# Attention with mixed heads: the products that form the softmax sums move from the front of a step's first mixing to its second quarter, and their reciprocals go behind the first transposition

## The chip, the cores and the metric

The kernel runs on one core of one Trainium2 chip. The metric is the device time of one execution in microseconds (us). The kernel before took 4113.27 us, the median of three runs that lie between 4112.35 and 4115.33 us.

## The reference, cut to what matters

Two attention layers work on x of shape 8 x 512 x 32 x 32, that is 8 images with 512 channels and 1024 positions. The change touches only the second layer:

```
q, k, v = w_q @ x, w_k @ x, w_v @ x            # 8 heads of 64 channels
attn = einsum('bhdq,bhdT->bhqT', q, k) * scale
attn = einsum('gh,bhqT->bgqT', w_head, attn)    # the heads are mixed
attn = softmax(attn, axis=-1)
mean, var = mean(attn), var(attn)               # over all queries and keys of a head
attn = (attn - mean) / sqrt(var + EPS) * in_gamma + in_beta
out  = einsum('bhqT,bhdT->bhqd', attn, v)       # then the projection w_proj
```

So for each query and head the kernel needs the sum of the exponentials (the softmax sum) and the sum of their squares (for var).

## The kernel before, in words

All data are float32. The first layer fills the span up to about 1800 us and is not touched. In the second layer the images follow one another, and each image has 8 blocks of 128 queries. A block passes through three stages, which lie in three successive steps; step p (p from 0 to 8, method `step`) works on three blocks at once and has four quarters, t = 0 to 3:

- Block p, scores (`scores`, L1631): eight products of queries and keys, two in each quarter. ScalarE copies each out of PSUM (L1643) into a tile `raw`, one tile for keys 0 to 511 (kh = 0) and one for keys 512 to 1023 (kh = 1). Then 16 DMAs of SyncE (`regroup`, L1648, 256 KB each) rearrange the rows into the tile `re`, so that all heads of 16 queries lie in 128 partitions. Slot s of `re` (s = 0 to 3) gets two DMAs for kh = 0 and two for kh = 1. They are issued in the order (kh, s) = (0,0), (0,1) in quarter 1, (0,2) in quarter 2, and (0,3), (1,0), (1,1), (1,2), (1,3) at the end of quarter 3. `re` has one buffer; `raw` has two.
- Block p-1, mixing (`mix`, L1665): four mixings, one a quarter, each 32 matmul records that read one slot of `re`. ScalarE takes the exponential of each in two halves into a tile `e` of 128 x 2048 (L1675; two buffers). VectorE transposes the tile (`flip`, L1687, into `et`) and takes mean and variance of each 512 columns (`moments`, four instructions of L1698). In quarter 3 the mixing stands ahead of the scores, in the other quarters behind them.
- Block p-2, values (`values`, L1714) from `et`: half 0 began in quarter 3 of the step before and ends in quarter 0; half 1 fills quarters 1 and 2. ScalarE moves each half out of PSUM (`leave`, L1730).

At the front of a step come the sums of block p-2. `sums` (three short VectorE instructions, L1740 to L1742) turns the 16 means and variances into the tile `zz`; its inputs are ready after the last `moments` of the step before. `totals` (L1749, two products, four matmul records) adds over the partitions into a PSUM tile `z`. `reciprocals` takes 1/z (L1760), keeps z (L1773), adds to the sum of squares (L1775 to L1780), and has GpSimd's queue write the reciprocals to DRAM (`zd`, L1763) and read them back spread over 64 partitions (`rzb`, L1770, 256 KB). GpSimd uses `rzb` two blocks later (`divide`, L1802).

The order of the work is written out by hand: every engine runs its instructions in the order in which the program emits them. On TensorE quarter 0 is thus: scores 0 and 1, second half of values half 0, `totals`, mixing 0. On VectorE: `sums`, `reciprocals`, `flip` 0, `moments` 0. An agenda (`ag.run`) puts other work at places that are numbered 4p + t: the next image's normalization in step 5, parts of the next key projection in step 8, where there are no new scores.

PSUM of this layer has three tiles of two banks (`m_psum`, for scores and mixings, in turn) and two of one bank (`acc_psum`, for the halves of values and for `z`, in turn). `totals` is called once a block; seven of an image's eight calls lie in `step` (56 in all), the eighth after the loop, and that one is not changed.

Of the kernel before, what the change touches and what calls it, by code (L numbers as in the profile page):

```python
# [467 lines left out]
def tile_two_attention_layers(  # L468
# [795 lines left out]
    with ExitStack() as l1:  # L1264
# [180 lines left out]
        def k_leave():  # L1445
            for fn in due:
                fn()
            due.clear()
# [167 lines left out]
        class Attention1:  # L1616
# [221 lines left out]
            def step(self, p, t, ag):  # L1838

                new, old, older = p < NT, p >= 1, p >= 2  # L1840
                if t == 3 and old:
                    self.mix(p - 1, 3)
                if new:
                    self.scores(p, 2 * t)
                    if t == 0:
                        self.scores(p, 1)
                if t == 0 and older:
                    self.values(p - 2, 0, 2, 3)
                    self.leave(p - 2, 0)
                    self.sums(p - 2)  # L1850
                    if p % 2 == 0 and p >= 4:
                        self.divide(p // 2 - 2, nc.gpsimd)
                    self.totals(p - 2)
                if t in (1, 2) and older:
                    self.values(p - 2, 1, t - 1)
                if t == 3 and old:
                    self.values(p - 1, 0, 0)
                if new and t:
                    self.scores(p, 2 * t + 1)
                if t == 3 and old:  # L1860
                    self.values(p - 1, 0, 1)
                if t < 3 and old:
                    self.mix(p - 1, t)
                ag.run(4 * p + t - 0.5)
                if t == 2 and older:
                    self.values(p - 2, 1, 2, 3)
                    self.leave(p - 2, 1)
                k_leave()
                if old:
                    self.flip(p - 1, t)  # L1870
                    self.moments(p - 1, t)
                if new:
                    for kh, s in (
                        (), ((0, 0), (0, 1)), ((0, 2),), ((0, 3), (1, 0), (1, 1), (1, 2), (1, 3)),
                    )[t]:
                        self.regroup(kh, s)
                if old and t == 0:
                    self.piece(4 if p < 5 else 5)
                ag.run(4 * p + t)
# [155 lines left out]
```

## Time and profile before

| what | value |
|---|---|
| median of the runs shown | 4113.27 us |
| the profiled execution, time | 4113.24 us |
| its span, first to last instruction | 4111.1 us |
| TensorE matmul busy | 3950.6 us (96%) |
| VectorE busy | 2832.7 us (69%) |
| ScalarE busy | 1970.3 us (48%) |
| GpSimd busy | 128.8 us (3%) |
| mean granted TensorE clock | 0.991 |
| DMA, SyncE's queue (q1) | 43.1% of the 16 engines over the span |

A group line of the profile gives line, engine, operation, output and inputs, shapes and count, then busy time, mean duration of one in ns, and the idle time of the engine just before the group with what ended most of it. A matmul of float32 appears as two records. The time outside the span is 2.1 us in the profiled execution, and it agrees with the median to 0.03 us.

### The profile page before, as it was taken

What the parts mean: (1) busy time and instruction counts of PE and PEld (TensorE: products, weight loads), DVE (VectorE), ACT (ScalarE), POOL (GpSimd) and SP (SyncE); (2) the same over time, 40 slices, a digit from 0 to 9 for tenths busy, and PEclk for the clock granted to TensorE, in tenths of its full rate; (3) what the DMA queues carried; (4) which work ended last, traced back from release to release, by engine and by line L of the source; (5) the groups of instructions that cost most, each with busy time, mean ns of one, the idle gap of its engine ahead of it and who ended that gap; (6) DMA issues with size and microseconds to landing.
All of it is one profiled execution on the core that took longest, in us unless ns stands there. A gap on an engine that the chain in (4) does not pass through costs nothing.

```text
span 4111.1 us, 96037 instructions
## 1 busy us (share of the span) xinstructions
PE 3950.6 (96%) x41932; PEld 1825.8 (44%) x41932; DVE 2832.7 (69%) x4124; ACT 1970.3 (48%) x2431; POOL 128.8 (3%) x150
## 2 busy tenths in 40 slices
PE   8999999999999999999999999999999999999997
PEld 4353535353534344334534544444444445444344
DVE  4748485757575666648758768668678588587586
ACT  1717272636354444427427347257166175274373
POOL 0000000000000000000000001000000000000000
PEclk9999999999999999999999999999999999999998
DMA  3313131212121111138649559468287286386484
GB/s 129 106 51 109 49 114 44 88 47 88 47 81 45 58 69 65 68 102 216 182 113 219 150 142 220 131 165 218 95 204 201 93 217 173 119 215 190 107 197 121
DMA packets 268636, 519.12 MB, mean 126 GB/s; under 512 B 49840, under 2 KB 84912, under 8 KB 261552
## 3 DMA queue, kind: packets, MB, share of 16 engines
q1 hardware_dynamic: 261664, 497.96, 43.1%
q0 software_dynamic: 6544, 14.94, 1.6%
q8 instruction: 331, 5.42, 0.6%
q14 instruction: 97, 0.79, 0.1%
HBM read 197.16 MB, written 46.92 MB: 59 GB/s over the span
## 4 chain that ended last, share of the span: by engine, by line
PE 71%; DVE 21%; ACT 3%; issue 2%; DMA 2%; SPq 0%; DVEq 0%; ACTq 0%
PE s L1081 11%; PE a L1107 10%; DVE bn L1698 10%; DVE et L1687 9%; PE pk_p L899 5%; PE pq_p L899 5%; PE pv L1458 5%; PE pv_p L899 5%; PE pp_p L899 5%; PE pk L1383 4%; PE pq L1383 4%; PE pp L1383 4%; PE a L1714 4%; PE s L1631 4%; PE m L1665 2%
## 5 line engine op out<-in xcount | busy, mean ns | idle before, releaser
L1687 DVE STREAM_TRANSPOSE et<-e 128x2048 f32<-128x2048 f32 x256 | 589.6, 2303 | 179.3 <-ACT e L1675 175.6
L1714 PEld LDWEIGHTS a<-et,v 128*64 128x64 f32 x16384 | 515.0, 140 | 296.8 <-issue 278.3
L1698 DVE BATCH_NORM_STATS2 bn<-e 128x6 f32<-128x512 f32 x1024 | 635.4, 685 | 0.0
L1675 ACT ACTIVATE e<-m 128x1024 f32<-128x1024 f32 x512 | 496.5, 1021 | 248.5 <-issue 157.7
L1086 ACT ACTIVATE e<-s 128x1024 f32<-128x1024 f32 x512 | 497.2, 1026 | 233.6 <-PE s L1081 232.2
L1643 ACT COPY raw<-s 128x1024 f32<-128x1024 f32 x480 | 478.2, 1017 | 226.9 <-PE s L1631 204.9
L1714 PE MATMUL a<-et,v 128*64 128x64 f32 x16384 | 563.7, 226 | 9.5 <-DVE et L1687 5.2
L1631 PE MATMUL s<-k,q 64*64 64x512 f32 x4096 | 547.7, 620 | 9.4 <-DVE q L1497 3.1
L1094 DVE TENSOR_TENSOR zacc<-zacc,e 128x1024 f32<-128x1024 f32 x384 | 468.6, 1220 | 89.9 <-ACT e L1086 67.9
L1081 PE MATMUL s<-q,k 64*64 64x512 f32 x4096 | 490.1, 593 | 2.3 <-ACT e L1086 2.3
L1107 PE MATMUL a<-e,v 64*64 64x512 f32 x4096 | 484.1, 589 | 0.0
L1665 PE MATMUL m<-re,wmix 32*32 32x512 f32 x8192 | 335.2, 610 | 5.9 <-ACT e L1675 3.4
L1107 PEld LDWEIGHTS a<-e,v 64*64 64x64 f32 x4096 | 156.7, 133 | 282.8 <-issue 282.5
L1081 PEld LDWEIGHTS s<-q,k 64*64 64x64 f32 x4096 | 147.9, 133 | 275.2 <-issue 240.7
L1631 PEld LDWEIGHTS s<-k,q 64*64 64x64 f32 x4096 | 119.0, 133 | 259.8 <-issue 103.5
L1458 PE MATMUL pv<-wv,y 128*128 128x512 f32 x480 | 212.1, 597 | 0.0
L1730 ACT COPY q<-a 64x256 f32<-64x256 f32 x256 | 93.9, 367 | 175.1 <-PE a L1714 173.0
L1763 POOL DMA_DIRECT2D zd<-rz x56 | 34.7, 619 | 3471.5 <-DMA re<-raw 1854.1
L1458 PEld LDWEIGHTS pv<-wv,y 128*128 128x128 f32 x480 | 89.3, 190 | 117.5 <-issue 109.5
L1665 PEld LDWEIGHTS m<-re,wmix 32*32 32x32 f32 x8192 | 69.0, 103 | 147.7 <-ACT raw L1643 87.5
L1462 ACT COPY v<-pv 128x512 f32<-128x512 f32 x30 | 17.6, 586 | 218.4 <-PE pv L1458 218.4
L1749 PE MATMUL z<-sel,zz 128*32 128x32 f32 x256 | 30.5, 208 | 94.6 <-DVE zz L1740 81.3
(315 smaller groups left out, 3993.3 us busy)
## 6 DMA issues: line engine op xcount, KB each, us to landing
re<-raw SPq DMA_DIRECT2D x1024, 256.0 KB
left_q<-left_q SPq DMA_DIRECT2D x17, 1792.0 KB
left_p<-left_p SPq DMA_DIRECT2D x17, 1792.0 KB
left_k<-left_k SPq DMA_DIRECT2D x10, 1792.0 KB
x<-in_x_dram SPq DMA_DIRECT2D x32, 512.0 KB
rzb<-zd SPq DMA_DIRECT2D x128, 128.0 KB
x<-x SPq DMA_DIRECT2D x64, 256.0 KB
left_v<-left_v SPq DMA_DIRECT2D x8, 1792.0 KB
```

Source lines behind the costliest of these rows:

```text
L899: nc.tensor.matmul(out, st, mv, start=start, stop=(k == 1), skip_group_check=True)
L1081: nc.tensor.matmul(ps[c * D : c * D + D, m], k[r, hp, k0 : k0 + D], q[r, hp, ts(f, FB)], start=True, stop=True,)
L1086: nc.scalar.activation(e[i], ps, AF.Exp, scale=S0 * S0)
L1107: nc.tensor.matmul(acc[g][a][m * D : m * D + D], v[rows, kc, ts(2 * hp + m, D)], e[i][rows, m], start=(kc == 0), stop=(kc == NG - 1),)
L1383: nc.tensor.matmul(self.ps[m][:, i], w[:, left, k * HC + i * P : k * HC + i * P + P], right[:, k], start=(k == 0 and m != 2), stop=(k == 1 ...
L1458: nc.tensor.matmul(ps[:, m], y_t[b][:, c, ts(2 * i + m, P)], w[:, c], start=(c == 0), stop=(c == NCC - 1),)
L1631: nc.tensor.matmul(ps[c * D : c * D + D, m], qo_t[b][r, p, hp, ts(c, D)], k_t[b][r, hp, ts(kh, FB)], start=True, stop=True,)
L1665: nc.tensor.matmul(ps[a // 2][c * 32 : c * 32 + 32, a % 2].rearrange("p (r kb k) -> p r kb k", r=2, k=32), wmix[rows].rearrange("p g i -> ...
L1675: nc.scalar.activation(e[:, :, 2 * h : 2 * h + 2].rearrange("p r a k -> p a r k"), ps[h].rearrange("p a (r k) -> p a r k", r=2), AF.Exp,)
L1687: nc.vector.transpose(self.et[p, u].rearrange("p kb (r st a) g q -> p st kb r (a g q)", r=2, st=2)[:, st], self.e[p, s].rearrange("p r a ( ...
L1698: nc.vector.bn_stats(self.bn[p][:, s, a], e[:, :, a].rearrange("p r k -> p k r"))
L1714: nc.tensor.matmul(acc[two * D : two * D + D, s].rearrange("p (x q) -> p x q", q=4), v_t[b][:, kb, ts(g, D)], et[:, kb, :, g], start=(kb = ...
```

## The change

`totals`, with the reciprocals that it calls, leaves quarter 0. It is called in quarter 1, after the first part of values half 1. The `flip` and `moments` of mixing 0 leave quarter 0 as well: `flip` 0 now stands ahead of `totals`, and `moments` 0 behind it. In step 1, which has no block p-2, both stay where they were. `sums` stays in quarter 0.

```diff
                     self.sums(p - 2)
                     if p % 2 == 0 and p >= 4:
                         self.divide(p // 2 - 2, nc.gpsimd)
-                    self.totals(p - 2)
                 if t in (1, 2) and older:
                     self.values(p - 2, 1, t - 1)
+                    if t == 1:
+                        self.flip(p - 1, 0)
+                        self.totals(p - 2)
+                        self.moments(p - 1, 0)
                 if t == 3 and old:
                     self.values(p - 1, 0, 0)
...
-                if old:
+                if p == 1 or old and t:
                     self.flip(p - 1, t)
                     self.moments(p - 1, t)
```

The resulting orders: TensorE has scores 0 and 1, values, mixing 0, score 2, the first part of values half 1, `totals`, score 3, mixing 1. VectorE has `sums`, `flip` 0, the four or five instructions of `reciprocals`, `moments` 0, `flip` 1. GpSimd's two DMAs for the reciprocals follow `totals`. No instruction is added or removed; what an agenda place of quarter 0 gives VectorE now comes ahead of `flip` 0. The two `acc_psum` tiles are now taken in the order half 0, half 1, `z` instead of half 0, `z`, half 1.

## The prediction

> **What bounds the kernel now.** I read the page first, then who waited for whom on TensorE, then one undisturbed block in the timelines of TensorE and VectorE, and the sums of that stretch. From the page, the span, the engines and the group of the moved products:
>
> ```profile
> span 4111.1 us, 96037 instructions
> PE 3950.6 (96%) x41932; PEld 1825.8 (44%) x41932; DVE 2832.7 (69%) x4124; ACT 1970.3 (48%) x2431; POOL 128.8 (3%) x150
> ...
> L1749 PE MATMUL z<-sel,zz 128*32 128x32 f32 x256 | 30.5, 208 | 94.6 <-DVE zz L1740 81.3
> ```
>
> TensorE is idle for 160.5 us of the span (4111.1 - 3950.6), and 94.6 us of it lie ahead of these few products, which are themselves 30.5 us. The waits of TensorE:
>
> ```profile
> PE z L1749 <- DVE zz L1740: 81.3, 53, 3.3
> PE z L1749 <- DVE zz L1742: 13.2, 55, 0.2
> ...
> PE m L1665 <- DMA re<-raw: 1.6, 6, 0.4
> ```
>
> The last line is small (6 waits, 1.6 us), and it is the one to distrust: a regrouped row that lands while TensorE waits for `zz` shows no wait of its own. TensorE's timeline (start, duration, record, idle before it) across one block, its plain middle left out:
>
> ```profile
> 3340.32 0.25 PE L1749 MATMUL z<-sel,zz 128*32 128x32 f32 x2 [1.29 <-DVE zz L1740]
> 3340.81 0.25 PE L1749 MATMUL z<-sel,zz 128*32 128x32 f32 x2 [0.24 <-DVE zz L1742]
> 3340.99 1.14 PE L1665 MATMUL m<-re,wmix 32*32 32x512 f32 x32
> 3342.06 1.10 PE L1631 MATMUL s<-k,q 64*64 64x512 f32 x8
> ...
> 3359.79 2.08 PE L1714 MATMUL a<-et,v 128*64 128x64 f32 x64
> 3363.16 0.25 PE L1749 MATMUL z<-sel,zz 128*32 128x32 f32 x2 [1.29 <-DVE zz L1740]
> ```
>
> The period is 22.84 us (3363.16 - 3340.32), of which TensorE runs without a gap for 20.88 (3340.99 to 3361.87) and is held for 1.96. Many blocks have this period to 0.03 us, which a chain of latencies would do. VectorE's timeline shows the chain:
>
> ```profile
> 3344.31 2.31 DVE L1687 STREAM_TRANSPOSE et<-e 128x2048 f32<-128x2048 f32 x1 [2.23 <-ACT e L1675]
> 3346.54 2.49 DVE L1698 BATCH_NORM_STATS2 bn<-e 128x6 f32<-128x512 f32 x4
> ...
> 3362.92 0.19 DVE L1740 TENSOR_SCALAR zz<-bn 128x32 f32<-128x32 f32 x1
> ```
>
> From 3344.31 on it runs four pairs of transposition and moments without a gap, then `zz`; then the two products, mixing 0 behind them, its exponential, and only then the next transposition. VectorE idles 2.23 us for that exponential, and TensorE for VectorE. Neither is full: in this stretch VectorE is busy 20.11 of 22.85 us. The DMA engines are fuller. In the sums of the stretch the busy times of TensorE, its weight loads, VectorE, ScalarE and GpSimd follow its length; the last three numbers are the granted clock, the DMA share and GB/s:
>
> ```profile
> 3340.99:3363.84 22.85, 21.28 (x455) 11.00 (x453) 20.11 (x28) 16.90 (x20) 3.53 (x3) 1.00 0.89 219
> ```
>
> [...] mixing 0 had its data at 3339.48 and started at 3340.99, behind `z`. [...] the first regroup transfer of a step lands 3.24 us after its issue (median of 29) when GpSimd's spread of reciprocals is not in flight, 4.84 us (27) when it is. [...]
>
> **The change, part by part.** I use the 56 blocks whose products move. The held time runs from the end of values to the first record of mixing 0; landings come from the times at which each DMA's semaphore rises in the trace.
>
> 1. *The wait for `zz` goes.* Over the 56 blocks TensorE is held 120.8 us in all (2.16 a block, the products themselves included). What is late next is the second transfer of slot (1,0), which mixing 0 reads: it is issued 3.30 us before the end of values in steps 3 to 7, and lands 3.78 us (median; mean 4.03) after that, so about 0.5 us too late (0.45 in the block above: values end at 3339.03, the landing is at 3339.48). In the six blocks where it was the releaser, mixing 0 began 0.13 us after the landing. Block by block, held time less (landing + 0.13 - end of values): the landing alone would hold TensorE for 67.5 us. Removed: 120.8 - 67.5 = 53.3 us. In step 8, without new scores, little is won (0.6 a block), since values end earlier and the landing is about 2.9 us away.
>
> 2. *The products at their new place.* In an image's eighth block they have no gap before them, and take 0.24 us from their start to the next record (2035.04 to 2035.28). Bounds: 0.2, and 0.67 as in the timeline above. They push the scores, and so the landing: 56 x 0.24 = 13.4 us lost. Their wait for `zz` is over by 2 us: mixing, score and values (3.2 us) lie between. The PSUM tile they take now was emptied ahead of mixing 0.
>
> 3. *Reciprocals ahead of moments 0.* Five instructions, 0.98 us (3341.10 to 3342.08). They delay moments 0, transposition 1 and moments 1. Behind them waits the fourth exponential, which needs the tile that moments 1 frees. Moments 1 ends 12.67 us after mixing 0 begins, with the insert at 13.62; the exponential, ready at 12.98 + 0.24 = 13.22, starts near 13.72. Of this 0.5 us about half reaches the eighth score's copy (ScalarE has slack there, the score ends later anyway), and so the regroup. 48 blocks (steps 3 to 8) x 0.25 = 12 us lost; bounds 0 and 0.6 a block. VectorE waits for no product: `z` is done 3.6 us after mixing 0, transposition 0 ends at 5.55.
>
> 4. *GpSimd's two DMAs move with them.* The write now starts 5.5 us later relative to mixing 0 (recips at 5.6 for 0.11). The spread's packets are in flight from 8.75 to 11.3 us after mixing 0 (medians), and would be from 14.2 to 16.8. Before, they met slots (0,0) to (0,2), with time to spare; now they meet (0,3), issued at 13 to 13.8, ahead of (1,0), issued near 17.5. Between the landing of (0,3) (17.9) and of (1,0)'s first transfer (20.3) lie 2.4 us, of which one transfer takes 1.1 (the spacing of landings in a full queue), so 1.3 are free; so the median is covered, the late quarter is not. Bounds: 0, and 1.6 us, the measured slowing (4.84 - 3.24). I take 0.2 on average: 48 x 0.2 = 9.6 us.
>
> 5. *The rest costs nothing.* `zz` is computed where it was; GpSimd's multiply follows a step later; SyncE's queue issues the same in the same order. Agenda work that now precedes transposition 0 (0.8 us of normalization in step 5, two subtractions of 1.22 us in step 8) fits into VectorE's wait for the exponential or, in step 8, beside TensorE's key projection (3.63 us a product); without that cover it would cost its own duration, 8 x 0.8 and 8 x 2.4 us. Half 0 of values now takes the PSUM tile that half 1 leaves, which is empty 0.9 us before. ScalarE's fifth copy waits for the regroup of (1,3), which lands 6.2 to 8.1 us after that of (1,0); the copy comes 7.6 us after mixing 0, nearly always later.
>
> Sum: 53.3 - 13.4 - 12 - 9.6 = 18.3 us. Against the profiled execution, 4113.24 - 18.3 = 4094.9, say 4095 us; the median shown is 0.03 us away. The plain block would go from 22.84 to 20.88 + 0.24 + 0.58 + 0.25 + 0.2 = 22.15 us.
>
> **The rivals.** *Cover holds (chance 0.20).* Parts 3 and 4 cost nothing: 4113.24 - 53.3 + 13.4 = 4073. For: VectorE has 2 us free and ScalarE 6 of 22.85. Against: moments 1 is late by the instructions' own durations.
>
> *Traded (0.20).* The regroup takes what `zz` gives back; the engines at 0.89 get fuller in a shorter period. If the landing comes 0.36 us later still (17.3/48), 4112. For: landings over 5 us occur already. Against: (1,0) finds the queue nearly empty.
>
> *Slower (0.15).* The reciprocals' spread runs into (0,3) and (1,0). Each hit costs 1.6 us; without part 4 the gain is 27.9 us, so it decides at 17 of 48 blocks, and above 23 the loss passes 0.2%. With three quarters hit, 36 x 1.6 = 57.6, less 27.9: 4143. For: 0.89, and the measured slowing. Against: at 16.8 the packets are mostly done.
>
> That the change does not do what it says is excluded: the orders of instructions are as described.
>
> **How the numbers follow.** My forecast has 0.45, centre 4095, 4084 to 4105. About 0.2% (8 us) is what a measurement can tell here. Faster by more: 0.45 + 0.20 = 0.65; within: 0.20; slower: 0.15. The range runs from 4066 (the covered case with shorter landings) to 4122; it leaves out the slower case and a little at the low end, together under 0.2.
>
> **What would show it.** Right: the wait of `z` for `zz` gone; mixing 0 waiting for the DMA instead, some 1 us a block; VectorE idle near 1.5 us ahead of transposition 0 and none after it; plain periods of 21.9 to 22.4 us; the fourth exponential waiting for moments. Wrong: periods of 22.8 or above with (1,0) landing over 4.7 us after issue (part 4); TensorE idle ahead of scores or values (a PSUM tile I took as free); no DMA wait at mixing 0 and periods near 21.2 (part 1 too pessimistic).

## The result and the profile after

| | before | after |
|---|---|---|
| median | 4113.6 us (4112.35 to 4115.33, 4 runs) | 4056.8 us (4052.18 to 4059.13, 4 runs) |
| ratio, 95% interval | | 0.986 (0.9843 to 0.9877) |
| profiled execution, time | 4113.24 us | 4059.13 us |
| its span, mean granted clock | 4111.1 us, 0.991 | 4057.0 us, 0.993 |

The change takes off 56.8 us, where 18 were forecast. It went the way that was expected, and further than the range of the prediction reaches (4066 to 4122 us).

From the page of the kernel after: the span, the engines, and the group of mixings, whose last two numbers are the idle time ahead of it and what ended most of it.

```profile
span 4057.0 us, 96037 instructions
PE 3927.5 (97%) x41932; PEld 1817.7 (45%) x41932; DVE 2834.4 (70%) x4124; ACT 1969.0 (49%) x2431; POOL 128.7 (3%) x150
...
L1665 PE MATMUL m<-re,wmix 32*32 32x512 f32 x8192 | 334.9, 611 | 72.6 <-DMA re<-raw 60.7
```

Two things are to be seen. The idle time that stood ahead of `z` now stands ahead of the mixings, and is smaller (94.6 before, 72.6 here). And TensorE's *busy* time fell by 23.1 us (3950.6 to 3927.5) although it runs the same 41932 instructions. 10.5 us of that are the `z` products themselves, whose records now follow each other without a gap (busy 30.5 us before, 20.1 here). The other 12.5 us lie in the records of scores and values: they became faster, and the prediction has no term for that.

The waits of TensorE after (total, count, longest). Those of `z` are gone:

```profile
PE m L1665 <- DMA re<-raw: 60.7, 45, 4.4
...
PE m L1665 <- ACT q L1730: 7.5, 9, 0.9
...
PE a L1714 <- issue: 0.6, 1, 0.6
```

The second line is a label to distrust. In the block below it names a ScalarE copy that ends at 3612.87; but the second transfer of slot (1,0) landed at 3612.75, and mixing 0 began 0.13 us after that, as it does where the profile names the DMA. So both lines are one wait: 68.2 us. Counted as in the prediction, TensorE is held 69.3 us in the 56 blocks, and the landings alone would hold it for 69.1.

TensorE's timeline over one plain block (start, duration, record, idle before it):

```profile
3590.97 1.15 PE L1665 MATMUL m<-re,wmix 32*32 32x512 f32 x32 [0.59 <-DMA re<-raw]
3592.05 1.09 PE L1631 MATMUL s<-k,q 64*64 64x512 f32 x8
3593.07 1.15 PE L1714 MATMUL a<-et,v 128*64 128x64 f32 x32
3594.15 0.31 PE L1749 MATMUL z<-sel,zz 128*32 128x32 f32 x4
3594.39 1.09 PE L1631 MATMUL s<-k,q 64*64 64x512 f32 x8
...
3610.00 2.08 PE L1714 MATMUL a<-et,v 128*64 128x64 f32 x64
3612.88 1.15 PE L1665 MATMUL m<-re,wmix 32*32 32x512 f32 x32 [0.80 <-ACT q L1730]
```

The products now run without a gap, 0.24 us from start to start (3594.15 to 3594.39). The period is 21.91 us (before 22.84). The sums of the stretch, with clock, DMA share and GB/s at the end, show the DMA engines a little fuller than before (0.91 against 0.89):

```profile
3590.97:3612.88 21.91, 21.07 (x452) 10.93 (x453) 19.84 (x29) 17.05 (x21) 3.51 (x3) 1.00 0.91 231
```

VectorE's timeline in the same block:

```profile
3592.16 0.22 DVE L1742 TENSOR_TENSOR zz<-zz,bn 128x32 f32<-128x32 f32 x1
3594.27 2.31 DVE L1687 STREAM_TRANSPOSE et<-e 128x2048 f32<-128x2048 f32 x1 [1.89 <-ACT e L1675]
3596.51 0.31 DVE L1760 RECIPROCAL rz<-z 32x32 f32<-32x32 f32 x1
...
3597.38 2.51 DVE L1698 BATCH_NORM_STATS2 bn<-e 128x6 f32<-128x512 f32 x4
3599.82 2.28 DVE L1687 STREAM_TRANSPOSE et<-e 128x2048 f32<-128x2048 f32 x1
```

The last `zz` ends at 3592.38, after mixing 0 has begun, and is wanted only at 3594.15. VectorE idles 1.89 us ahead of transposition 0 and no more after it. ScalarE's fourth exponential waits for `moments`, 13.65 us after mixing 0 began (3604.62 - 3590.97):

```profile
3604.62 1.94 ACT L1675 ACTIVATE e<-m 128x1024 f32<-128x1024 f32 x2 [0.83 <-DVE bn L1698]
```

### The profile page after: what moved, and what is told of

It is laid out like the page before. It is cut to its first block, busy times and chain, and to the rows that moved or that the text cites. A ratio compares the mean times of both kernels' runs of the same rounds, so it can differ in the third digit from the quotient of the medians.

```text
span 4057.0 us, 96037 instructions
## 1 busy us (share of the span) xinstructions
PE 3927.5 (97%) x41932; PEld 1817.7 (45%) x41932; DVE 2834.4 (70%) x4124; ACT 1969.0 (49%) x2431; POOL 128.7 (3%) x150
## 5 line engine op out<-in xcount | busy, mean ns | idle before, releaser
L1665 PE MATMUL m<-re,wmix 32*32 32x512 f32 x8192 | 334.9, 611 | 72.6 <-DMA re<-raw 60.7
L1462 ACT COPY v<-pv 128x512 f32<-128x512 f32 x30 | 17.6, 585 | 218.4 <-PE pv L1458 218.4
L1092 DVE TENSOR_TENSOR zacc<-e,e 128x1024 f32<-128x1024 f32 x64 | 78.3, 1223 | 55.3 <-ACT e L1086 55.3
```

The costliest lines, as they stand in the source:

```text
L1665: nc.tensor.matmul(ps[a // 2][c * 32 : c * 32 + 32, a % 2].rearrange("p (r kb k) -> p r kb k", r=2, k=32), wmix[rows].rearrange("p g i -> ...
```

## The experiments

The first theory was that the step periods (from one mixing 0 to the next) shrink because the wait for `zz` goes, and that parts 3 and 4 of the prediction cost less than forecast. The rival was that something else than the wait had gone. "Held" below is the sum over the 56 blocks from the end of values to mixing 0; a "pass" is the rest of the period, from mixing 0 to the end of values in the next step. Held time, passes, waits and stretches of half clock are those of the one profiled execution of each kernel. Ratios are to the kernel before on the same chip, whose medians there were 4117.6 us for the first four kernels, 4114.5 for the next four and 4116.4 for the last two.

**1. The products alone move.** The transposition and the moments of mixing 0 stay in quarter 0, so VectorE runs them both ahead of the reciprocals. Against the kernel after:

```diff
                     if t == 1:
-                        self.flip(p - 1, 0)
                         self.totals(p - 2)
-                        self.moments(p - 1, 0)
...
-                if p == 1 or old and t:
+                if old:
```

> Only the products move to quarter 1; transposition 0 and moments 0 stay in quarter 0, so VectorE has the reciprocals behind moments 0. Theory (mixing 0 is now held only by the landing of slot (1,0), and VectorE's order counts little): 4049 to 4065 us, held time ahead of mixing 0 near 69 us over the 56 blocks. Rival (the reordering on VectorE carries a good part of the gain): above 4075 us.

Measured: 4062.5 us, ratio 0.986 (0.9845 to 0.9875), span 4059.4, held 75.4 us. The ratio is that of the kernel after, and the wait for the landing is still the one that holds TensorE:

```profile
PE m L1665 <- DMA re<-raw: 70.4, 49, 4.3
```

The gain comes with the move of the products (and of the reciprocals behind them); whether the reciprocals stand ahead of moments 0 or behind adds nothing that can be measured.

**2. The reciprocals one pair later**, behind moments 1:

```diff
-                self.reciprocals(p, ps)
+                self.zps = ps
...
+                if t == 1 and older:
+                    self.reciprocals(p - 2, self.zps)
...
```

> As the changed kernel, but the reciprocals stand behind moments 1 on VectorE. It measures part 3 of the prediction. If the reciprocals delay the fourth exponential and with it the regroup by 0.2 us in each of 48 blocks: about 10 us less than the changed kernel (4042 to 4052), the fourth exponential no longer waiting for moments. If that delay is covered in most blocks: within 4 us of the changed kernel.

Measured: 4085.4 us (five runs, 4075.0 to 4097.7), ratio 0.993 (0.9917 to 0.9944), held 91.8 us in the fastest of them. Neither expectation came: it is slower than the kernel after. The fourth exponential hardly waits for the moments any more (the second fence: ScalarE's waits; in the kernel after 38.8 us in 44), yet TensorE is held longer:

```profile
PE m L1665 <- DMA re<-raw: 85.9, 49, 4.3
```

```profile
ACT e L1675 <- DVE bn L1698: 11.8, 10, 2.0
```

Putting the reciprocals later also puts GpSimd's spread later, by about 5 us, into the transfers of slot (1,0): in steps 3 to 8 the second of them lands 4.4 to 4.8 us after its issue (means by step), in the kernel after 3.8 to 4.3. This is the mechanism of the rival "Slower". Here it costs some 23 us (4085.4 against 4062.5 of the first experiment on the same chip); in the kernel after the spread lies some 5 us ahead of it.

**3. No spread, products at the new place.** `rzb` is filled once an image with ones, and the DMA that spreads the reciprocals is left out, so values aren't divided by their softmax sums:

```diff
-                if p % 2 == 0:
+                if p == 0:
                     self.rzb = zpool.tile([P, T], F32, tag="rzb", name=f"rzb_{b}_{p}")
-                h = p % 2 * D
-                queue.dma_start(
-                    out=self.rzb[h : h + D], in_=zd.rearrange("g i -> (g i)").partition_broadcast(D)
-                )
+                    nc.gpsimd.memset(self.rzb, 1.0)
```

> As the changed kernel, but the read of the reciprocals from DRAM that spreads them over the partitions is left out; the tile is set to one at each image's first block, so the values are not divided by the softmax sums. It measures part 4 of the prediction. Theory (the spread does not reach slot (1,0)): within 6 us of the changed kernel, second transfer of (1,0) landing 3.8 to 4.0 us after issue as before. Rival (it costs the predicted 0.2 us a block or more): 10 us or more below the changed kernel.

Measured: 4046.9 us, ratio 0.9824 (0.981 to 0.9837), held 64.5 us. The spread costs 11 to 15 us in all (0.986 less 0.9824 is 0.0036 of 4117 us, 15; the spans differ by 11.2). That is the size that the rival expected. Of the 11.2, 4.8 us are held time, 2.2 are shorter passes, and 2.7 lie behind the last block, where the output waits for it.

**4. The reciprocals ahead of transposition 0.** The products go to the front of quarter 1, the transposition behind them, which takes part 3 of the prediction away, since VectorE idles there anyway:

```diff
                 if t in (1, 2) and older:
-                    self.values(p - 2, 1, t - 1)
                     if t == 1:
-                        self.flip(p - 1, 0)
                         self.totals(p - 2)
+                        self.flip(p - 1, 0)
                         self.moments(p - 1, 0)
+                    self.values(p - 2, 1, t - 1)
```

> As the changed kernel, but the products stand ahead of the first part of values half 1, and the reciprocals ahead of transposition 0, in VectorE's idle time before it (about 1.9 us in the changed kernel). Theory: the reciprocals then cost nothing, so the same as with the reciprocals late, 0 to 10 us below the changed kernel. Rival (VectorE waits for the products and transposition 0 starts late): TensorE idle ahead of the products, 5 us or more above it.

Measured: 4062.2 us, ratio 0.9863 (0.9848 to 0.9878), held 65.2 us. The waits of TensorE, then those of ScalarE:

```profile
PE m L1665 <- DMA re<-raw: 58.9, 46, 4.2
...
PE a L1714 <- issue: 6.4, 6, 2.1
```

```profile
ACT e L1675 <- DVE bn L1698: 12.0, 10, 2.0
```

The edit does what it should: the exponential's waits fall from 38.8 to 12.0 us. But held time falls by only 4.1 (69.3 to 65.2). The time doesn't fall at all, because the passes of this kernel are 12.5 us longer: 11.1 us of TensorE's time in them is at half clock, and values stand still six times for 6.4 us with nothing in the profile that they wait for. Both of these also appear in the kernel before. The first led to experiment 6; on the second, experiment 7 has something to say.

**5. The kernel after, once more.**

> The changed kernel itself, for comparison with the others on the same chip: ratio to the kernel before 0.984 to 0.988, held time ahead of mixing 0 between 66 and 76 us.

Measured: 4054.5 us, ratio 0.9849 (0.983 to 0.9868), span 4054.0; held 69.3 us again, passes 1171.0 (1174.7 in the first profile). So held time repeats, and passes scatter by a few us.

**6. The kernel before, its wait filled.** TensorE does idle products while it waits for `zz`, ahead of the sums' own, into a part of the PSUM tile that nobody reads:

```diff
                 ps = acc_psum(f"z1_{self.b}_{p}")
+                for m in range({0: 3, 3: 1, 4: 2, 6: 4}.get(p, 0)):
+                    nc.tensor.matmul(
+                        ps[:, P:FB], ones, v_t[self.b][:, m, P:FB], start=True, stop=True,
+                    )
```

> The kernel before, with idle products of 384 columns [...] ahead of the products for the sums, into unused columns of their PSUM tile: three for an image's first block, one for its fourth, two for its fifth, four for its seventh. TensorE then works through part of the wait for zz. Theory (in the kernel before, waits of about 2 us and more were followed by stretches at half clock, and their going is part of the gain): the half-clock stretches inside the steps fall from seven to two or fewer and the time by 4 to 12 us. Rival (those stretches come by themselves, whatever TensorE waits for): their number stays, the time is the same or up to 8 us more.

Measured: 4099.0 us, ratio 0.9957 (0.9941 to 0.9973). The span and the clock of this kernel (the clock before is 0.991):

```profile
core 0: 4091.4 us, clock 0.998
```

It adds work and takes 15.5 us off, more than the 4 to 12 that were expected. The wait itself is still there, since the plain block still has its period of 22.84 us and the held time is 124.8 us; the products only fill it (three of them take 2.20 us), and TensorE's longest idle time ahead of the sums' products falls from 3.3 to 1.3 us. What changed is the clock. In the second layer of the kernel before (1850 us to the end of values) there are 13 stretches, of 3.4 or 6.8 us, in which TensorE was granted half its clock; here there is one. What such a stretch does is seen in the kernel before. Two neighbouring blocks (length, busy times of the engines, then clock, DMA share, GB/s):

```profile
2441.88:2465.84 23.96, 23.06 (x454) 11.79 (x452) 20.03 (x27) 16.89 (x20) 1.15 (x2) 0.93 0.82 198
2465.84:2488.68 22.84, 21.29 (x455) 11.00 (x453) 20.09 (x28) 16.90 (x20) 3.52 (x3) 1.00 0.92 228
```

and TensorE's timeline at the start of the first:

```profile
2441.21 0.25 PE L1749 MATMUL z<-sel,zz 128*32 128x32 f32 x2 [2.09 <-DVE zz L1740]
...
2443.06 1.99 PE L1631 MATMUL s<-k,q 64*64 64x512 f32 x8
2444.97 1.69 PE L1714 MATMUL a<-et,v 128*64 128x64 f32 x32
```

There is a wait of 2.09 us, and soon after it eight score records take 1.99 us instead of 1.09, and 32 of values 1.69 instead of 1.15. The block is 1.12 us longer, and the clock column shows 0.93. Of the 13 stretches nine begin 0.9 to 2.1 us behind the end of a wait of 1.3 to 3.1 us, and four begin inside a wait of 3.3 to 5.2 us (the last section counts which waits have a stretch behind them).

Not all of this gain can be set beside the change. Of the 19.7 us between the two profiled spans (4111.1 and 4091.4), 6.9 lie in the 56 periods (the passes are 10.9 us shorter, the held time 4.0 longer), 8.2 between mixing 0 of step 8 and the next image's first mixing, 3.4 ahead of the first mixing and the rest at the end. The change leaves 3.21 us of hold in step 8 (mean; 3.77 before), and gains nothing outside the periods.

**7. The kernel before without its spread**, the edit of experiment 3 (values are again not divided).

> The kernel before without the read that spreads the reciprocals (the tile is set to one, so the values are not divided by the softmax sums). Theory (at its old place the spread was hidden; only its new place costs): within 5 us of the kernel before, some 3 us of it from the last block's end. Rival (the spread costs the same wherever it lies): 10 us or more below the kernel before, as it was for the changed kernel.

Measured: 4111.15 us, ratio 0.9989 (0.9982 to 0.9995), held 131.8 us, passes 1166.0 us (1180.8 with the spread).

```profile
PE z L1749 <- DVE zz L1740: 93.1, 56, 3.3
```

In time the spread costs 3.3 us at the old place, as the theory had it; the stretch behind the last block is 3.1 us shorter. At the new place it costs 11 to 15. But inside the steps more has moved: the passes are 14.8 us shorter, and the wait for `zz` takes 11.0 of that back (93.1 us, 81.3 before), since the chain on VectorE sets the period, and the plain block still takes 22.84 us. About 4 of the 14.8 us are half clock, by the comparison of passes that follows in the next section. With the rest go the short stalls amid values for which the profile names nothing: the kernel before has eight of them, this one none. So the spread at its old place did cost time in the passes, and the wait for `zz` hid it.

**8. Cover for the landing.** The first part of values half 1 moves ahead of mixing 0, so that TensorE has 1.08 us of work while (1,0) lands; the reciprocals go ahead of transposition 0, as in experiment 4:

```diff
                     if p % 2 == 0 and p >= 4:
                         self.divide(p // 2 - 2, nc.gpsimd)
+                    self.values(p - 2, 1, 0)
                 if t in (1, 2) and older:
-                    self.values(p - 2, 1, t - 1)
                     if t == 1:
-                        self.flip(p - 1, 0)
                         self.totals(p - 2)
+                        self.flip(p - 1, 0)
                         self.moments(p - 1, 0)
+                    else:
+                        self.values(p - 2, 1, 1)
```

> A version that fills the wait for slot (1,0): the first part of values half 1 (1.08 us) ahead of mixing 0, the products ahead of transposition 0 in quarter 1 and the reciprocals ahead of it. Theory (mixing 0 is held by the landing only, and TensorE has other work): held time below 35 us over the 56 blocks, plain period 21.1 to 21.4 us, 20 to 40 us below the changed kernel. Rival (VectorE's chain of transpositions and moments takes over as the limit): plain period still near 21.9, within 10 us of the changed kernel.

Measured: 4032.4 us, ratio 0.9799 (0.9781 to 0.9817), held 15.7 us. TensorE's wait for the landing, and one of ScalarE's (9.4 us in 21 in the kernel after):

```profile
PE m L1665 <- DMA re<-raw: 18.1, 17, 2.2
```

```profile
ACT e L1675 <- ACT raw L1643: 33.4, 75, 0.5
```

Held time falls by 53.6 us and the kernel by 22, which is within the theory's 20 to 40. The plain block gains only 0.26 us (21.91 to 21.65): from the start of mixing 1 to the next scores now pass 1.87 us instead of 1.20. So the period misses the theory's 21.1 to 21.4: the pass gets a wait of its own as soon as the hold is gone. Most of the gain lies in step 8, whose hold falls from 3.2 to 1.5 us (14 us for eight images), and behind it, where the half-clock stretches go (three left in the layer, of eight).

**9. A key product earlier.** In step 8 of the kernel after, TensorE is held 3.21 us for the landing (mean), and in six of the eight images a half-clock stretch begins in that wait or just behind it. The next image's key projection, 3.63 us a product, stands behind that; its first product moves ahead:

```diff
-                ag.at(4 * NT - 0.5, lambda: right_tile(b + 1))
-                ag.at(4 * NT - 0.5, lambda: k_go(1))
+                ag.at(4 * NT - 1, lambda: right_tile(b + 1))
+                ag.at(4 * NT - 1, lambda: k_go(1))
```

> The changed kernel with the next image's first key product (3.6 us of TensorE) at the end of step 7 in place of behind mixing 0 of step 8. In the changed kernel the longest waits for slot (1,0), some 3 us, lie there, and half-clock stretches follow them. Theory (landing and clock): the wait in step 8 goes in seven of eight images (about 3.2 us each, 22 us in all), and the half-clock stretches behind it go too (up to 1.7 us each, some 10 us): 20 to 32 us below the changed kernel. Rival (other work is late there as well, or the clock falls by itself): less than 12 us.

Measured: 4032.5 us, ratio 0.9795 (0.9782 to 0.9808), clock 0.996. The hold of step 8 falls from 3.21 to 0.59 us, which is 21 us for eight images: nearly the whole gain of 22 to 24 us over the kernel after (4054.5 and 4056.8 us). The half-clock stretches fall from eight to four, but the further 10 us that were expected of that can't be seen.

**10. Both: the key product, and a score product ahead of mixing 0 as cover.**

```diff
-                if new:
+                if new and t != 1:
                     self.scores(p, 2 * t)
...
+                if new and t == 0:
+                    self.scores(p, 2)
                 if t in (1, 2) and older:
                     self.values(p - 2, 1, t - 1)
                     if t == 1:
-                        self.flip(p - 1, 0)
                         self.totals(p - 2)
+                        self.flip(p - 1, 0)
                         self.moments(p - 1, 0)
```

and the two lines of experiment 9.

> As the one before, and in the other steps score 2 (1.02 us) ahead of mixing 0, with the reciprocals ahead of transposition 0. Unlike the version that moved values there, the first exponentials and the copies of scores 2 and 3 keep their distance from mixing 1. Theory: held time below 20 us over the 56 blocks, plain period 21.1 to 21.4 us, 50 to 70 us below the changed kernel. Rival (the next limit, ScalarE's copies or VectorE, is as near as in that version): plain period 21.6 or more, less than 45 us below.

Measured: 4031.2 us, ratio 0.9794 (0.9781 to 0.9808), held 10.5 us (0.19 a block) when the score product that now stands there is taken off. The wait of TensorE for the landing, and the one of ScalarE that took its place (27.6 us in 20 in the kernel after):

```profile
PE m L1665 <- DMA re<-raw: 9.1, 9, 4.2
```

```profile
ACT raw L1643 <- DMA re<-raw: 43.2, 30, 3.1
```

Nothing is won over experiment 9: it is some 23 us below the kernel after, where the theory had 50 to 70 and the rival less than 45. The fifth score copy of a block now comes so early that it waits for the regroup of slot (1,3), which frees `raw`; mixing 2 then stands 1.6 to 2.1 us ahead of values in many blocks, where 1.09 is the undisturbed distance. Experiments 8 to 10 each beat both kernels, and lie within 1.3 us of each other.

## Why the prediction was wrong in size

The profiled pair differs by 54.1 us, where 18.3 were forecast. Two steps failed. Parts 3 and 4 were to make the landing's hold 21.6 us longer; it became 1.6 us longer (67.5 to 69.1). And the passes were taken as given but for the products; in fact they lost 17.6 us of half clock and stalls, for which the prediction has no term. No run shows a common cause, so that both err to the same side passes for chance. The 56 periods show where the missing 36 us are:

| term | forecast | measured | missing |
|---|---|---|---|
| held time, 120.8 to 69.3 | -31.7 (-53.3 + 12 + 9.6) | -51.5 | 19.8 |
| passes, 1180.8 to 1174.7 | +11.5 (48 products) | -6.1 | 17.6 |
| outside the 56 periods | +1.9 (8 products) | +3.6 | -1.7 |

*Part 1, the wait for `zz`: right in mechanism, incomplete as a sum.* What is late next is the landing of (1,0), as said: 69.3 us held, 69.1 by the landing. But the step took "120.8 - 67.5 = 53.3" as all that goes with the wait, and the passes as given. That is the step that failed on the side of the passes, and two things were in them.

The first is the clock. A pass in which TensorE slows was in the profile of before, and I took no notice of it: the stretches at half clock in the 56 passes fall from 25.1 to 4.4 us, and passes with such a stretch were longer than the others of the same step by 11.6 us in sum before and by 2.3 after. About 9 of the 17.6 us are that, and experiment 6 shows on the kernel before that filling the waits is enough to bring the clock back (0.991 to 0.998; passes 10.9 us shorter).

The second is the spread. Some 8 us remain, and short stalls amid values, for which the profile names nothing, are part of them. The list of waits of the kernel before has this line (in the kernel after it is 0.6 us in one, in experiment 5 there is none):

```profile
PE a L1714 <- issue: 4.3, 8, 1.0
```

They don't hang on the wait for `zz`: experiment 4 has them with that wait gone (6.4 us in 6), experiment 7 has none with the wait still there. They go with GpSimd's spread. There are none in the two kernels without it (experiments 3 and 7). Where it is issued 6.7 to 8.5 us after mixing 0 (medians) there are eight, seven and six (before, experiments 6 and 4), though only one in experiment 8 and three in experiment 10; where it is issued some 11 us after or later there are none or one (after, experiments 1, 2, 5 and 9). The prediction says of the spread's old place that it met the transfers there "with time to spare", and so put at nothing what it cost there. How the spread makes TensorE stall was not tested.

*Part 2, the products: right.* 0.24 us each, and the undisturbed pass goes from 20.88 to 21.12 us.

*Part 3, the reciprocals ahead of moments 0: over-sized.* The exponential starts 13.65 us after mixing 0, forecast 13.72, so the delay is there. But taking part 3 away (experiment 4) frees 4 us of held time, not 12. "About half reaches the eighth score's copy" failed: the issue of (1,0) moved from 3.30 to 3.12 us ahead of the end of values in the transitions into steps 4 and 5, and hardly in the others. There TensorE itself is later (the second half of mixing 2 waits for the fifth score copy), and moves the end of values along with the issue.

*Part 4, GpSimd's DMAs: about right in sum, in part by luck.* 11 to 15 us against 9.6. But the 9.6 were to be held time, and of that it is 4.8; the rest lies in the passes and behind the last block. What the spread cost at its old place is missing (above). Its packets are in flight 13.2 to 15.7 us after mixing 0 (medians; 14.2 to 16.8 forecast), which is why (1,0) mostly escapes them.

Parts 3 and 4 together were to raise the landing's hold from 67.5 to 89.1 us; it is 69.1. Experiments 3 and 4 account for 4 to 5 us each, so that without both it would be about 60, not 67.5. In the three kernels with the order of before it is 67.5, 63.4 and 64.5 in one execution each, so scatter is some 4 us of this. About 3 to 7 us stay open.

*Part 5: right.* No new wait ahead of scores or values, and the `z` products wait for nothing.

*The rivals.* "Cover holds" came nearest (4073), and still lies 16 us too high, which is about the passes' share. "Traded" didn't happen: on the mean (1,0) doesn't land later after its issue (3.99 us, before 4.03). "Slower" didn't either, but experiment 2 shows its place some 5 us further on.

## What to carry to other kernels

When a wait on the bounding engine goes, ask not only what is late next, but also what the wait itself did to the engine: compare steps of one kind with each other, and look at the clock column and at the busy time of a record of one shape. Here waits of some two microseconds cost clock on top of the waiting, so that even useless work in them paid: the granted clock went from 0.991 to 0.998, and the time fell by 15.5 us (experiment 6). While a chain on another engine set the period, what slowed the bounding engine by less than its wait mostly shortened the wait, and hardly showed in the time (experiment 7: passes 14.8 us shorter without the spread, 11.0 of them taken back by the wait). And a DMA that moves with its producer needs its own place: at the old one the spread cost time in the passes, 5 us further on than in the kernel after it costs 23 us.

## What was not expected of the hardware

- In the second layer of the kernel before, nine of the 13 stretches at half clock, of 3.4 or 6.8 us, stand behind waits of only 1.3 to 3.1 us, and one stretch in all is left once the waits are filled (experiment 6, clock 0.998). Many waits of the same length are followed by none (53 waits for `zz` in all, up to 3.3 us). The profiles of the kernels before and after let one count when they come. In each of the two the stretches start whole multiples of 3.4133 us apart (to 0.01 us). I cut both, from 1850 us to the end of values, into windows of that length and added up TensorE's idle time in each window at full clock, by the ends that the profile gives for its records. After all 15 windows with 2.0 us or more the clock is halved (seven before, eight after), after 6 of the 23 with 1.5 to 2.0 us, and after none of the 1216 with less. So two waits of 2.09 us in the kernel before differ: the window of the one that ends at 2441.21 has 2.08 us of idle time, and half clock follows at 2442.80; the one that ends at 2733.72 is shared between two windows, with 1.30 and 1.03 us of idle time in them, and none follows. Ahead of 1850 us one stretch doesn't fit: it starts at 1835.22 us (1835.65 after), behind a window without idle time. What sets the clock was not tested. After the change the stretches sit nearly all in step 8 and behind it, where the landing is waited for 3.21 us (mean), and in experiment 10 two are left (clock 0.997).
- TensorE stands still for up to 2.1 us (experiment 4) amid a run of values, with no semaphore behind it. The kernels before and after have eight such stalls and one in the 56 passes, of 0.2 to 1.0 us, and each ends 1.3 to 1.7 us after the end of a transfer in the queue that the page calls `instruction` (q8), whose transfers start 7.1 and 6.6 us apart (medians). That would fit instructions that come late, and was not tested. The stalls go when GpSimd's spread is left out (none in experiments 3 and 7), and nearly so when it comes late (one in the kernel after); whether the spread holds up such transfers, no run shows. One stall of the kernel before:

```profile
2457.15 0.50 PE L1714 MATMUL a<-et,v 128*64 128x64 f32 x9
2458.09 0.92 PE L1714 MATMUL a<-et,v 128*64 128x64 f32 x23 [0.44 <-issue]
```
